# New tiling of a ConvNeXt block and a selective scan: sixteen-tile convolutions, tiled MLP, scan units of 1568 tokens

## The chip, the core and the metric

The kernel runs on one core of one Trainium2 chip. The metric is the time of one execution in microseconds (us) on the device. Engines are written as in the profile: PE (matrix engine; PEld is its weight load), DVE (vector), ACT (scalar/activation), POOL (GpSimd), SP (the queue that issues most DMAs). SBUF is the working memory of 128 partitions, PSUM the small memory that PE writes into, DRAM the large memory outside.

## The reference

The input `x` is 32 images of 96 channels, 56 by 56, in float32. Two layers follow each other:

```python
# layer 0
h = depthwise_conv7x7(x) + conv_b                       # per channel
h = (h - mean_c(h)) * rsqrt(var_c(h) + 1e-5) * g + b     # over the 96 channels
h = gelu(h @ w1 + b1) @ w2 + b2                          # 96 -> 384 -> 96
x = h * layer_scale + x
# layer 1, L = 3136 tokens per image, N = 4, R = 6
xs = silu(depthwise_conv5x5(x) + conv_b)
dts, Bs, Cs = split(x_proj_w @ xs)                       # 6, 4, 4 rows
delta = softplus(dt_w @ dts + dt_b)                      # 96 x L
log_dA = maximum(delta * A, log(1e-9))                   # 96 x 4 x L
P = exp(cumsum(log_dA)); dB_u = delta * Bs * xs
hs = P * cumsum(dB_u / maximum(P, 1e-9))
y = sum_n(hs * Cs) + xs * Ds
```

## The kernel before

The kernel has four stages, one after the other; each stage leaves its result in DRAM and the next one loads it.

**Convolution 1 (96 steps, one per channel).** `convolve` (L191) puts 112 image rows (2 half-batches of 56 rows) on the partitions and 16 images of 56 columns along the free side. The vertical part of the 7x7 filter is a banded 112x112 matrix, loaded for each channel from `taps_d` (L196); the horizontal part is seven shifted matmuls for each of two halves of 448 columns (L212). ACT adds the bias (L238), POOL's queue stores the result, and DVE with ACT accumulates the channel sums and squares (L245 to L248). After the last channel DVE and ACT make `rstd`, which goes to DRAM.

**MLP (112 steps, one per image row).** SP loads 96x896 tiles of the convolution, of `rstd` and of `x`; DVE multiplies by `rstd` (L273); PE does three times two matmuls into `ph` (L278), ACT the Gelu (L286), PE three times two matmuls into `po` (L293), DVE the residual sum (L301).

**Convolution 2** is like convolution 1 with five taps and a Silu (L316).

**Scan (384 units).** A unit is 784 tokens of one image (a quarter) times 32 of the 96 channels times 4 states, that is 128 partitions. An order written out by hand and pinned (`pin`) interleaves the steps of neighbouring units. `spread_du` copies 32 rows of `du` four times with four DMAs (L415, from SBUF to SBUF); `decay` makes the decay factor on ACT in three passes (L424 to L426); `drive` (L431) and `weigh` (L458) are products on POOL, `delta_x` (L392) a third one per quarter image; `scan` runs three operations on DVE: a scan into `run` (L439), a `min` and product in place in `run` (L446), and a second scan (L450). `gather` sums the states on PE (L468), `store` copies the result out on ACT (L477) and SP stores it. These lines decide where the DVE's operands lie (`ps_k` is a pool in PSUM):

```python
pv = ps_k.tile([128, 1024], F32, name="pv")
nc.vector.memset(pv, 0.0)
zero = pv[:, 1023:1024].to_broadcast([128, CH])
run = pv[:, :CH]
```

Of the kernel before, what the change touches and what calls it, by code (L numbers as in the profile page):

```python
# [15 lines left out]
B2, BI = 2, 16  # L16
ROWS = B2 * H
COLS = BI * W
HALF = COLS // 2
# [4 lines left out]
WP = 2 * H - 1  # L24
CH = 784
NCH = L // CH
BK = CH // 2
LN_EPS = 1e-5
EPS = 1e-9
DG = C // 3  # L30
# [4 lines left out]
def convnext_then_scan_kernel(  # L35
# [22 lines left out]
    nc = tc.nc  # L58
    const = ctx.enter_context(tc.tile_pool(name="const", bufs=1))
    dram = ctx.enter_context(tc.tile_pool(name="dram", bufs=1, space=DRAM))  # L60


    conv1_d = dram.tile([C, ROWS, COLS], F32, name="conv1_d")
    block_d = dram.tile([C, ROWS, COLS], F32, name="block_d")
    conv2_d = dram.tile([C, ROWS, COLS], F32, name="conv2_d")
    rstd_d = dram.tile([ROWS, COLS], F32, name="rstd_d")
    taps1_d = dram.tile([C, WP * K1], F32, name="taps1_d")
    taps2_d = dram.tile([C, WP * K2], F32, name="taps2_d")

# [5 lines left out]
    def across(src, parts, n, name):  # L75
        t = const.tile([parts, n], F32, name=name)
        nc.sync.dma_start(t, src.rearrange("(o n) -> o n", o=1).to_broadcast([parts, n]))
        return t


# [5 lines left out]
    nc.gpsimd.memset(lift_t[:, 0:1], -EPS)  # L86
    nc.gpsimd.memset(lift_t[:, 1:2], EPS)

    c1b_t = across(c1b, ROWS, C, "c1b_t")
    c2b_t = across(c2b, ROWS, C, "c2b_t")  # L90
    g_t = column(ln_g, C, "g_t")
    lnb_t = column(ln_b, C, "lnb_t")
    b2_t = column(b2, C, "b2_t")
    ls_t = column(ls, C, "ls_t")
    ls_b = across(ls, 128, C, "ls_b")
    dtb_t = column(dtb, C, "dtb_t")
    ds_t = column(ds, C, "ds_t")
    w1_t = const.tile([C, F], F32, name="w1_t")
    nc.sync.dma_start(w1_t, w1)
# [4 lines left out]
    xp_t = const.tile([R, C], F32, name="xp_t")  # L104
    nc.sync.dma_start(xp_t, xp[:R, :])
    xpT_t = const.tile([C, R + 2 * N], F32, name="xpT_t")
    nc.sync.dma_start(xpT_t, xpT)
    dtwT_t = const.tile([R, C], F32, name="dtwT_t")
    nc.sync.dma_start(dtwT_t, dtwT)
    a_t = const.tile([128, NG], F32, name="a_t")  # L110
    for n in range(N):
        nc.sync.dma_start(
            a_t[n * DG : (n + 1) * DG, :],
            alog[n * C : (n + 1) * C].rearrange("(g p) -> p g", p=DG),
        )

    w1c_t = const.tile([C, F], F32, name="w1c_t")
    b1p_t = const.tile([128, 3], F32, name="b1p_t")
    b2p_t = const.tile([C, 1], F32, name="b2p_t")
    wd_t = const.tile([C, C], F32, name="wd_t")  # L120
    bcw_t = const.tile([C, 32], F32, name="bcw_t")
    pick_t = const.tile([128, 128], F32, name="pick_t")
    sel_t = const.tile([128, DG], F32, name="sel_t")
    dsm_t = const.tile([C, C], F32, name="dsm_t")

    with tc.tile_pool(name="prep", bufs=1) as prep, tc.tile_pool(
        name="prep_ps", bufs=1, space=PSUM
    ) as prep_ps:

        for taps_d, cw, k, flip in ((taps1_d, c1w, K1, False), (taps2_d, c2w, K2, True)):  # L130
            kt = prep.tile([C, k * k], F32, name=f"kt{k}")
            nc.sync.dma_start(kt, cw)
            pad = prep.tile([C, WP * k], F32, name=f"pad{k}")
            nc.vector.memset(pad, 0.0)
            at = (H - 1 - k // 2) * k
            if flip:
                for i in range(k):
                    j = k - 1 - i
                    nc.vector.tensor_copy(
                        pad[:, at + i * k : at + (i + 1) * k], kt[:, j * k : (j + 1) * k]  # L140
                    )
            else:
                nc.vector.tensor_copy(pad[:, at : at + k * k], kt)
            nc.sync.dma_start(taps_d, pad)


        cen = prep.tile([C, C], F32, name="cen")
        nc.vector.tensor_scalar(cen, ident[:C, :C], -1.0 / C, None, ALU.add)
        w1g = prep.tile([C, F], F32, name="w1g")
        nc.vector.tensor_scalar(w1g, w1_t, g_t, None, ALU.mult)  # L150
        ps = prep_ps.tile([C, 512], F32, name="ps_w1")
        nc.tensor.matmul(ps[:, :F], lhsT=cen, rhs=w1g, start=True, stop=True)
        nc.vector.tensor_copy(w1c_t, ps[:, :F])
# [7 lines left out]

# [4 lines left out]
        ps = prep_ps.tile([C, 512], F32, name="ps_wd")  # L166
        nc.tensor.matmul(ps[:, :C], lhsT=xp_t, rhs=dtwT_t, start=True, stop=True)
        nc.vector.tensor_copy(wd_t, ps[:, :C])


        nc.vector.memset(bcw_t, 0.0)
        nc.vector.tensor_copy(bcw_t[:, : 2 * N], xpT_t[:, R:])
        nc.vector.memset(pick_t, 0.0)
        for k in range(4):
            rows = slice(32 * k, 32 * k + 2 * N)
            for n in range(N):
                at = 32 * k + (k // 2) * N + n
                nc.vector.tensor_copy(
                    pick_t[rows, n * DG : (n + 1) * DG],
                    ident[rows, at : at + 1].to_broadcast([2 * N, DG]),  # L180
                )
        for n in range(N):
            rows = slice(n * DG, (n + 1) * DG)
            nc.vector.tensor_copy(sel_t[rows], ident[rows, rows])
# [3 lines left out]

    def convolve(src, taps_d, k, pool, psum, wts, c, load):  # L191
        wt = wts[c % len(wts)]
        for j in range(B2):
            rows = slice(j * H, (j + 1) * H)
            taps = bass.AP(taps_d.tensor, taps_d.offset + c * WP * k, [[k, H], [1, H * k]])
            load.dma_start(  # L196
                wt[rows, j * H * k : (j + 1) * H * k],
                taps,
            )
# [21 lines left out]
    def two(t):  # L221
        return t.rearrange("p (s q) -> p s q", s=2)
# [341 lines left out]
```

## Time and profile before

| | us |
|---|---|
| median of 3 runs | 5092.57 (5092.25 to 5094.79) |
| span of the profiled execution, first to last instruction | 5088.6 |
| PE busy / DVE busy / ACT busy / POOL busy | 4048.3 / 2414.6 / 2311.2 / 1786.0 |
| first matmul of convolution 1, of the MLP, of convolution 2 | 23.9, 1032.1, 2054.6 |
| first DVE scan | 2797.8 |

For the profiled execution only its span is listed, not a time of its own; the span lies 4.0 us below the median. Busy times are unions: where matmuls overlap, PE is counted once. A line of the profile's groups reads: line, engine, operation, output from inputs by their names, shapes, count, then busy time, mean duration of one in ns, and the idle time just before with what ended it. DMA share is the mean busy share of 16 DMA engines. Every float32 matmul of the program appears as two records (4608 for the 2304 of L212); such a record is called a pass below.

### The profile page before, as it was taken

How to read it: one execution, taken by the hardware profiler on the slowest of the kernel's cores; microseconds unless marked ns; L12 is line 12 of the kernel's file. 1: busy time of each engine (PE TensorE's matmuls, PEld its weight loads, DVE VectorE, ACT ScalarE, POOL GpSimd, SP SyncE). 2: the span in 40 equal slices, each digit the busy share in tenths (PEclk: the TensorE clock that was granted, in tenths of full speed). 3: DMA queues.
4: the chain of work that ended last, by engine and by line, in shares of the span. 5: the costliest groups of instructions: out<-in, count | busy, mean ns of one | idle time of the engine just before them, and what ended most of it. 6: DMA issues, size and time to landing. Idle time of an engine off the chain costs nothing.

```text
span 5088.6 us, 38136 instructions
## 1 busy us (share of the span) xinstructions
PE 4048.3 (80%) x11914; PEld 2152.7 (42%) x11914; DVE 2414.6 (47%) x2004; ACT 2311.2 (45%) x2547; POOL 1786.0 (35%) x1209
## 2 busy tenths in 40 slices
PE   8999999989999999999998555555555555555555
PEld 6777777644444444677775111111111111111111
DVE  2333333322222222000000788778877787778878
ACT  1111111233333333111112777777777777777776
POOL 0000000000000000000001676767766676767766
PEclk9999999999999999999999777777777777777777
DMA  3333333255555544344445787777877787778875
GB/s 91 95 98 94 99 93 100 79 161 152 155 154 152 154 152 133 114 129 126 125 128 128 168 174 170 164 169 171 175 160 169 166 176 167 163 168 173 174 165 127
DMA packets 375571, 726.55 MB, mean 143 GB/s; under 512 B 220600, under 2 KB 242200, under 8 KB 375368
## 3 DMA queue, kind: packets, MB, share of 16 engines
q1 hardware_dynamic: 352840, 608.48, 52.0%
q0 software_dynamic: 22528, 115.62, 5.7%
q8 instruction: 95, 1.56, 0.1%
q14 instruction: 108, 0.88, 0.1%
HBM read 260.59 MB, written 155.05 MB: 82 GB/s over the span
## 4 chain that ended last, share of the span: by engine, by line
PE 21%; POOL 10%; DMA 7%; ACT 7%; DVE 5%; SPq 5%; issue 5%; POOLq 0%; ACTq 0%; DVEq 0%
PE ps L212 14%; DMA rep<-du 7%; POOL hc L458 5%; SPq L415 5%; POOL u L431 4%; PE pn L383 2%; PE py L468 2%; PE py L365 2%; DVE pv L439 2%; DVE hs L450 2%; ACT da L424 1%; ACT da L425 1%; DVE pv L446 1%; ACT L424 1%; POOL du L392 1%
## 5 line engine op out<-in xcount | busy, mean ns | idle before, releaser
L212 PE MATMUL ps<-xt,wt 112*112 112x440 f32 (+3 forms) x4608 | 1692.2, 530 | 21.0 <-DMA xt<-in_x_dram 11.3
L212 PEld LDWEIGHTS ps<-xt,wt 112*112 112x112 f32 x4608 | 1262.7, 274 | 450.3 <-issue 27.8
L365 PE MATMUL py<-xs,dsm_t 96*96 96x392 f32 x512 | 373.3, 884 | 842.9 <-ACT y L477 842.9
L431 POOL TENSOR_TENSOR u<-rep,bt 128x784 f32<-128x784 f32 x384 | 713.0, 1857 | 663.3 <-ACT bt L406 595.7
L458 POOL TENSOR_TENSOR hc<-hs,ct 128x784 f32<-128x784 f32 x384 | 712.1, 1854 | 9.9 <-DVE hs L450 9.9
L439 DVE TENSOR_TENSOR_SCAN pv<-da,cp,pv 128x784 f32<-128x784 f32 x288 | 534.2, 1855 | 375.3 <-ACT da L426 354.3
L286 ACT ACTIVATE g<-ph,b1p_t 128x896 f32<-128x896 f32 x336 | 338.7, 1008 | 676.1 <-PE ph L278 676.1
L365 PEld LDWEIGHTS py<-xs,dsm_t 96*96 96x96 f32 x512 | 122.4, 269 | 1047.5 <-ACT y L477 952.2
L468 PE MATMUL py<-hc,sel_t 128*32 128x392 f32 x1536 | 535.7, 571 | 16.7 <-POOL hc L458 16.7
L278 PE MATMUL ph<-h,w1c_t 96*128 96x448 f32 x1344 | 525.6, 540 | 25.2 <-DVE h L273 25.2
L450 DVE TENSOR_TENSOR_SCAN hs<-da,hs,pv 128x784 f32<-128x784 f32 x288 | 532.0, 1847 | 10.3
L293 PE MATMUL po<-g,w_t 128*96 128x448 f32 x1344 | 523.6, 539 | 0.0
L273 DVE TENSOR_TENSOR h<-h,r 96x896 f32<-96x896 f32 x112 | 121.8, 1088 | 734.4 <-DMA h<-conv_d 720.6
L304 POOL DMA_DIRECT2D block_d<-o x112 | 57.6, 514 | 980.5 <-DVE o L301 932.8
L446 DVE SCALAR_TENSOR_TENSOR pv<-pv,u 128x784 f32<-128x784 f32 x384 | 377.4, 983 | 40.8 <-DVE cp L444 0.5
L424 ACT ACTIVATE da<-rep,a_t 128x784 f32<-128x784 f32 x384 | 364.3, 949 | 67.5 <-DMA rep<-du 58.3
L245 DVE TENSOR_TENSOR dt<-ht,first 112x896 f32<-112x896 f32 x95 | 103.8, 1093 | 580.2 <-ACT ht L238 580.2
L278 PEld LDWEIGHTS ph<-h,w1c_t 96*128 96x128 f32 x1344 | 255.7, 190 | 279.8 <-issue 279.8
L241 POOL DMA_DIRECT2D conv_d<-ht x95 | 50.1, 527 | 919.9 <-ACT ht L238 919.9
L425 ACT ACTIVATE da<-da,lift_t 128x784 f32<-128x784 f32 x384 | 364.9, 950 | 12.5
L426 ACT ACTIVATE da<-da,lift_t 128x784 f32<-128x784 f32 x384 | 364.9, 950 | 12.5
L316 ACT ACTIVATE st<-ps,c2b_t 112x896 f32<-112x896 f32 x96 | 96.7, 1008 | 601.9 <-PE ps L212 601.9
(74 smaller groups left out, 2905.1 us busy)
## 6 DMA issues: line engine op xcount, KB each, us to landing
rep<-du SPq DMA_DIRECT2D x1536, 196.0 KB
xt<-in_x_dram SPq DMA_DIRECT2D x96, 392.0 KB
h<-conv_d SPq DMA_DIRECT2D x112, 336.0 KB
r<-rstd_d SPq DMA_DIRECT2D x112, 336.0 KB
x<-in_x_dram SPq DMA_DIRECT2D x112, 336.0 KB
block_d<-o POOLq DMA_DIRECT2D x112, 336.0 KB, 4.3
xt<-block_d SPq DMA_DIRECT2D x96, 392.0 KB
conv_d<-st POOLq DMA_DIRECT2D x96, 392.0 KB, 4.4
```

The lines of the kernel that those rows point to most:

```text
L212: nc.tensor.matmul(pv[:, :, lo:hi], lhsT=wv[:, :, kw], rhs=xv[:, s * (BI // 2) : (s + 1) * (BI // 2), lo + dx : hi + dx], start=(i == 0), ...
L278: nc.tensor.matmul(ph[:, s, :HALF], lhsT=w1c_t[:, f * 128 : (f + 1) * 128], rhs=ht[:, s * HALF : (s + 1) * HALF], start=True, stop=True,)
L293: nc.tensor.matmul(po[:, s, :HALF], lhsT=w2_t[:, f, :], rhs=gs[f][:, s * HALF : (s + 1) * HALF], start=(f == 0), stop=(f == 2),)
L365: pin(nc.tensor.matmul(ps[:, s, :BK], lhsT=wt, rhs=xt[:, s * BK : (s + 1) * BK], start=start, stop=stop,))
L424: pin(nc.scalar.activation(da, reps[i][:, 0, :], AF.Exp, scale=a_t[:, g : g + 1]))
L425: pin(nc.scalar.activation(da, da, AF.Relu, bias=lift_t[:, 0:1], scale=1.0))
L431: pin(nc.gpsimd.tensor_mul(ut, reps.pop(i)[:, 1, :], bts[i // NG]))
L439: pin(nc.vector.tensor_tensor_scan(run, da, zero, carry["p", g] if q else 1.0 / EPS, ALU.mult, ALU.add))
L446: pin(nc.vector.scalar_tensor_tensor(run, in0=run, scalar=1.0, in1=ut, op0=ALU.min, op1=ALU.mult))
L450: pin(nc.vector.tensor_tensor_scan(ht, da, run, carry["h", g] if q else 0.0, ALU.mult, ALU.add))
L458: pin(nc.gpsimd.tensor_mul(hc, done.pop(i), cts[i // NG]))
L468: pin(nc.tensor.matmul(pys[k][g * DG : (g + 1) * DG, s, :BK], lhsT=sel_t, rhs=hc[:, s * BK : (s + 1) * BK], start=False, stop=True, tile_p ...
```

## The change

All four stages get another tiling.

- **Convolutions:** 48 tiles instead of 96 channels. A tile is 8 images (one of 4 groups, `g`) times 8 channels (`kb`). PE is addressed as 16 tiles of 32 by 32: row tile `i` holds 31 input rows of a half image and a row of ones for the bias, column tile `j` another channel. For each tap there are 16 matmuls with `tile_position`. The filter matrices of all 12 `kb` are loaded once, by `weights`, with 96 DMAs on ACT's queue in each convolution; each second one overwrites the last row of what the one before it wrote. The input tile is loaded by eight DMAs of 16 or 15 partitions each.
- **Statistics** stay in SBUF (`rstd_t`) and are spread over partitions by a matmul (`rb`).
- **MLP:** 56 units of four image rows of 8 images. The first product is done as 32x128 row tiles (three thirds `e` of the channels accumulate), the second as 128x32 column tiles.
- **Scan:** 192 units of 1568 tokens. `fetch` loads the spread `delta` and `delta*x` from DRAM with two DMAs of 128 partitions, after `delta` and `delta_x` wrote them there; `decay` has two ACT passes instead of three; every product writes over one of its inputs; `run` and the zero operand lie in SBUF.

The core of the diff:

```diff
+    def weights(t, taps_d, bias_d, k, n, kb, zs):
+        for i in range(Q):
+            cp, h = divmod(i, 2)
+            c0 = kb * 8 + cp
+            pin(nc.scalar.dma_start(
+                t[i * PR : (i + 1) * PR],
+                at(taps_d, c0 * n * k + zs[h] * k, [[k, PR], [2 * n * k, Q], [1, PR * k]]),
+            ))
+            pin(nc.scalar.dma_start(
+                t[i * PR + PR - 1 : (i + 1) * PR],
+                at(bias_d, c0 * PR * k, [[PR * k, 1], [2 * PR * k, Q], [1, PR * k]]),
+            ))
+
+    def convolve(ps, xt, wt, k):
...
+            for i in range(Q):
+                rows = slice(i * PR, (i + 1) * PR)
+                for j in range(Q):
+                    cols = slice(j * PR, (j + 1) * PR)
+                    pv = ps[cols, i, :COLS].rearrange("p (b w) -> p b w", w=W)
+                    pin(nc.tensor.matmul(
+                        pv[:, :, lo:hi],
+                        lhsT=wv[rows, j, :, kw],
+                        rhs=xv[rows, j, :, lo + dx : hi + dx],
+                        start=(t == 0),
+                        stop=(t == k - 1),
+                        tile_position=(i * PR, j * PR),
+                    ))
...
+        wts = []
+        for kb in range(KB):
+            wt = keep.tile([128, Q, PR * K1], F32, name=f"wt1_{kb}")
+            weights(wt, taps1_d, bias1_d, K1, T1, kb, (3, 0))
+            wts.append(wt)
+        xts = [keep.tile([128, Q, COLS], F32, name=f"x1_{i}") for i in range(4)]
...
+            for i in range(Q):
+                cp, h = divmod(i, 2)
+                for lo, hi in pieces():
+                    row = g * H + h * LOW + lo
+                    pin(nc.sync.dma_start(
+                        xt[i * PR + lo : i * PR + hi],
+                        at(x, ((kb * 8 + cp) * ROWS + row) * COLS,
+                           [[COLS, hi - lo], [2 * ROWS * COLS, Q], [1, COLS]]),
+                    ))
+        for n in range(B2 * KB):
+            g, kb = divmod(n, KB)
+            if n + 3 < B2 * KB:
+                load1(n + 3)
+            ps = psum.tile([128, Q, 512], F32, name=f"ps1_{n}", tag="ps")
+            convolve(ps, xts[n % len(xts)], wts[kb], K1)
+            ht = pool.tile([128, Q, COLS], F32, name=f"ht_{n}", tag="ht", bufs=3)
+            pin(nc.scalar.copy(ht, ps[:, :, :COLS]))
+            sq = pool.tile([128, Q, COLS], F32, name=f"sq_{n}", tag="sq")
+            pin(nc.scalar.activation(sq, ht, AF.Square))
...
+            for q in range(Q):
+                m = o * Q + q
+                rows = slice(q * PR, (q + 1) * PR)
+                for e in range(3):
+                    pin(nc.sync.dma_start(
+                        ht[rows, e].rearrange("p h w -> p (h w)"),
+                        at(conv1_d[g], (e * 16 * PR + m) * SLOT,
+                           [[PR * SLOT, 16], [2 * COLS, 2], [1, 2 * COLS]]),
+                    ))
...
+            for e in range(3):
+                for q in range(Q):
+                    rows = slice(q * PR, (q + 1) * PR)
+                    pin(nc.tensor.matmul(
+                        ph[:, q, :COLS], lhsT=w1c_t[rows, e, f * 128 : (f + 1) * 128],
+                        rhs=ht[rows, e, h], start=(e == 0), stop=(e == 2),
+                        tile_position=(q * PR, 0),
+                    ))
+            gt = pool.tile([128, Q, COLS], F32, name=f"g_{u}_{f}", tag="g", bufs=6)
+            pin(nc.scalar.activation(
+                gt, ph[:, :, :COLS], AF.Gelu, bias=b1p_t[:, f : f + 1], scale=1.0
+            ))
...
+                for q in range(Q):
+                    rows = slice(q * PR, (q + 1) * PR)
+                    pin(nc.tensor.matmul(
+                        po[rows, e, :COLS], lhsT=w2_t[:, f, e * PR : (e + 1) * PR],
+                        rhs=gts[u, f][:, q], start=(f == 0), stop=(f == 2),
+                        tile_position=(0, q * PR),
+                    ))
...
-        pv = ps_k.tile([128, 1024], F32, name="pv")
-        nc.vector.memset(pv, 0.0)
-        zero = pv[:, 1023:1024].to_broadcast([128, CH])
-        run = pv[:, :CH]
...
+            pin(nc.sync.dma_start(dl_d[k], dl))
...
-        def spread_du(i):
-
+            for i, (home, name) in enumerate(((bts, "bt"), (cts, "ct"))):
+                pk = psum.tile([128, Q, 512], F32, name=f"pk_{k}_{i}", tag="bc")
+                spread(pk, pick_t[:, i, :], k, 128)
+                t = pool.tile([128, T], F32, name=f"{name}_{k}", tag=name)
+                pin(nc.scalar.copy(four(t), pk[:, :, :BK]))
+                home[k] = t
+
+        def fetch(i):
             k, g = divmod(i, NG)
-            rep = pool.tile([128, 2, CH], F32, name=f"rep_{i}", tag="rep", bufs=4)
-            for n in range(N):
-                pin(nc.sync.dma_start(
-                    rep[n * DG : (n + 1) * DG], dus[k][g * DG : (g + 1) * DG]
-                ))
-            reps[i] = rep
+            da = pool.tile([128, T], F32, name=f"da_{i}", tag="da", bufs=6)
+            ut = pool.tile([128, T], F32, name=f"u_{i}", tag="u", bufs=6)
+            for t, d in ((da, dl_d[k]), (ut, dx_d[k])):
+                pin(nc.sync.dma_start(t, at(d, g * PR * T, [[T, PR], [0, N], [1, T]])))
+            das[i], us[i] = da, ut
 
         def decay(i):
-
-            k, g = divmod(i, NG)
-            da = pool.tile([128, CH], F32, name=f"da_{i}", tag="da", bufs=5)
-            pin(nc.scalar.activation(da, reps[i][:, 0, :], AF.Exp, scale=a_t[:, g : g + 1]))
-            pin(nc.scalar.activation(da, da, AF.Relu, bias=lift_t[:, 0:1], scale=1.0))
-            pin(nc.scalar.activation(da, da, AF.Identity, bias=lift_t[:, 1:2], scale=1.0))
-            ready[i] = da
+            da, g = das[i], i % NG
+            pin(nc.scalar.activation(
+                da, da, AF.Relu, bias=lift_t[:, 0:1], scale=a_t[:, g : g + 1]
+            ))
+            pin(nc.scalar.activation(da, da, AF.Exp, bias=lift_t[:, 1:2], scale=1.0))
 
         def drive(i):
-            ut = pool.tile([128, CH], F32, name=f"u_{i}", tag="u", bufs=5)
-            pin(nc.gpsimd.tensor_mul(ut, reps.pop(i)[:, 1, :], bts[i // NG]))
-            ready[i] = ready[i], ut
+            pin(nc.gpsimd.tensor_mul(us[i], us[i], bts[i // NG]))
 
         def scan(i):
             k, g = divmod(i, NG)
-            q = k % NCH
-            da, ut = ready.pop(i)
-
+            q = k % 2
+            da, ut = das[i], us[i]
+            run = pool.tile([128, T], F32, name=f"run_{i}", tag="run", bufs=1)
             pin(nc.vector.tensor_tensor_scan(
                 run, da, zero, carry["p", g] if q else 1.0 / EPS, ALU.mult, ALU.add
             ))
-            if q < NCH - 1:
+            if q == 0:
                 cp = pool.tile([128, 1], F32, name=f"cp_{i}", tag=f"cp{g}")
-                pin(nc.vector.tensor_copy(cp, run[:, CH - 1 : CH]))
+                pin(nc.vector.tensor_copy(cp, run[:, T - 1 : T]))
                 carry["p", g] = cp
             pin(nc.vector.scalar_tensor_tensor(
-                run, in0=run, scalar=1.0, in1=ut, op0=ALU.min, op1=ALU.mult
-            ))
-            ht = pool.tile([128, CH], F32, name=f"hs_{i}", tag="hs", bufs=5)
+                ut, in0=run, scalar=1.0, in1=ut, op0=ALU.min, op1=ALU.mult
+            ))
             pin(nc.vector.tensor_tensor_scan(
-                ht, da, run, carry["h", g] if q else 0.0, ALU.mult, ALU.add
-            ))
-            carry["h", g] = ht[:, CH - 1 : CH]
-            done[i] = ht
+                ut, da, ut, carry["h", g] if q else 0.0, ALU.mult, ALU.add
+            ))
+            carry["h", g] = ut[:, T - 1 : T]
...
         def weigh(i):
-            hc = pool.tile([128, CH], F32, name=f"hc_{i}", tag="hc", bufs=3)
-            pin(nc.gpsimd.tensor_mul(hc, done.pop(i), cts[i // NG]))
-            done[i] = hc
-
-        def gather(i):
-            k, g = divmod(i, NG)
+            pin(nc.gpsimd.tensor_mul(das[i], us.pop(i), cts[i // NG]))
+            hcs[i] = das.pop(i)
```

The main loop of the scan now does, at step `i`: `fetch(i + 4)`, `decay(i + 2)`, `drive(i + 2)`, `scan(i)`, `weigh(i - 1)`, `gather` of unit `i - 2`.

## Prediction

> **What bounds the kernel now.** I read the stages first: four windows cut at the first matmul of each stage and the first DVE scan.
>
> ```profile
> core 0: us, PE busy (x) PEld busy (x) DVE busy (x) ACT busy (x) POOL busy (x), PEclk, DMA share, GB/s
> 0.00:1032.00 1032.00, 986.67 (x2698) 747.56 (x2698) 331.80 (x337) 192.27 (x196) 51.57 (x105) 0.99 0.33 94
> 1032.00:2055.00 1023.00, 1013.17 (x2689) 475.08 (x2690) 249.01 (x227) 338.71 (x336) 57.59 (x112) 1.00 0.49 151
> 2055.00:2798.00 743.00, 728.61 (x1988) 523.86 (x1987) 1.08 (x2) 110.66 (x113) 61.67 (x102) 0.98 0.45 126
> 2798.00:5088.60 2290.60, 1319.85 (x4540) 406.25 (x4540) 1832.71 (x1440) 1669.56 (x1903) 1615.21 (x890) 0.74 0.77 167
> ```
>
> In the first three stages PE is busy 96 to 99% at full clock and everything else at most half: PE is the bound. The scan has no engine that is always busy; DVE comes first with 1832.7 of 2290.6. There DVE and POOL together are busy 3447.9 us, so for at least 1157 us both work at once. The groups by line give the price of each operation:
>
> ```profile
> L212 PE MATMUL ps<-xt,wt 112*112 112x440 f32 (+3 forms) x4608 | 1692.2, 530 | 21.0 <-DMA xt<-in_x_dram 11.3
> ...
> L431 POOL TENSOR_TENSOR u<-rep,bt 128x784 f32<-128x784 f32 x384 | 713.0, 1857 | 663.3 <-ACT bt L406 595.7
> L458 POOL TENSOR_TENSOR hc<-hs,ct 128x784 f32<-128x784 f32 x384 | 712.1, 1854 | 9.9 <-DVE hs L450 9.9
> L439 DVE TENSOR_TENSOR_SCAN pv<-da,cp,pv 128x784 f32<-128x784 f32 x288 | 534.2, 1855 | 375.3 <-ACT da L426 354.3
> ...
> L278 PE MATMUL ph<-h,w1c_t 96*128 96x448 f32 x1344 | 525.6, 540 | 25.2 <-DVE h L273 25.2
> L450 DVE TENSOR_TENSOR_SCAN hs<-da,hs,pv 128x784 f32<-128x784 f32 x288 | 532.0, 1847 | 10.3
> ...
> L446 DVE SCALAR_TENSOR_TENSOR pv<-pv,u 128x784 f32<-128x784 f32 x384 | 377.4, 983 | 40.8 <-DVE cp L444 0.5
> ```
>
> Matmul passes overlap, so I use busy time over count: 1692.2/4608 = 0.367 us per pass in the convolutions, 525.6/1344 = 0.39 in the MLP (0.375 where nothing waits: the timeline has runs of 12 passes in 4.67 us, 11 x 0.375 and one whole pass of 0.54). In the scan rows look at the operands: each of the three DVE operations has one of its two tensors in `pv`, which is PSUM, even the zero of L439. Last, two stretches of the timeline (start, duration, what). The first, of the scan, shows whether tiles of PE run side by side; `pk` is four row tiles, `py` a column tile:
>
> ```profile
> 4009.61 0.94 PE L400 MATMUL pk<-bn,pick_t 8*128 8x392 f32 x8
> ...
> 4010.49 0.86 PE L468 MATMUL py<-hc,sel_t 128*32 128x392 f32 x4
> ```
>
> The second, of the start, shows what it costs when a DMA waits for another to land:
>
> ```profile
> 15.07 0.79 SPq L144 DMA_DIRECT2D taps_d<-pad  x2
> 17.69 0.74 SPq L196 DMA_DIRECT2D wt<-taps_d  x2
> ```
>
> Eight passes in four row tiles take 0.94 us, where one after the other they would take 8 x 0.33 = 2.6. Sixteen passes of `pn` in four column tiles (L383, at 4049.81) take 2.75 us at a low clock, against 5.2 at the full one. So tiles overlap four-fold, both ways; of sixteen at once there is no row.
>
> **The change, stage by stage.** I call one set of passes that run side by side a round.
>
> *Convolution 1.* Now 2688 passes x 0.367 = 987 us on PE. After: 48 tiles x 7 taps x 2 passes = 14 rounds of 0.367 = 5.1 us per tile, if 16 tiles overlap as 4 do. The other engines per tile: ACT one copy (L406: 807 ns for 784 columns, so under 1.9 for 1792) and a Square (952 ns for 896, under 1.9), DVE four additions of 896 (1093 ns each, 4.4 us), all below the DMA. A tile loads 0.89 MB and stores 0.92 MB. Two rows give the rate at full DMA share: 94/0.33 = 285 GB/s where a transfer covers 112 partitions, 167/0.77 = 217 in the scan, where `rep` goes into 32. The packets agree: 6272 bytes of `rep` take 239 ns at the 5th percentile, but 479 in the median. The new loads cover 16 or 15 partitions; no row shows that. Bounds per tile: 1.81 MB at 285 = 6.3 us; loads at half of 217 (8.2) plus store at 285 (3.2) = 11.4. I take 9.0, nearer to the `rep` row, with the store mostly beside the loads. PE then idles part of the time; at the clock of 0.74 that the scan row grants it would need 6.9 us, still hidden. The skill's page "SBUF — State Buffer", section "Door 1: The DMA port swizzle", lists 104 GB/s for partitions 0 to 15; by it the loads alone would be an estimated 8.5 us.
>
> New, and on the path: the 96 weight DMAs stand on ACT's queue ahead of the first copy, and each second one overwrites a row of the one before, so it waits for its landing. The row: issue 0.37, then 1.83 us from the end of the `taps_d` issue to the next that waits for it, then 0.37: 2.6 us a pair, 48 pairs = 125 us (2.2 to 3.0 a pair: 106 to 144). Behind them wait ACT's copies, and PE, which has two PSUM buffers and stops after two tiles. The `x` loads on SP hide under it. Sum: 24 lead-in (as now) + 125 + 47 x 9.0 + 26 lead-in of the MLP (as now) + 12 for three rounds of statistics = **610** (464 to 742), now 1032.
>
> *MLP.* Per unit 9 rounds for the first and 9 for the second product, two passes each: 36 passes x 0.375 = 13.5, `rb` 0.75. Six changes between row and column tiles: above, 0.88 us pass from the first `pk` to the next `py` where two rounds are 0.65, so 0.1 to 0.23 each; I take 0.15 = 0.9. That is 15.1 us x 56 = 846, + 10 to the next stage = **856** (805 to 884), now 1023. ACT's Gelu (under 2.0 us) has `ph` in one buffer and hides under the other product's 2.2 us; without that cover it would add 3 x 2 us per unit, 336 us. DMA: 4.1 MB per two units at 217 GB/s = 19 of 30 us, hidden.
>
> *Convolution 2.* PE 10 rounds, 3.7 us; DMA as above. The weights' DMAs now wait on ACT behind the last Gelu and for the buffers of the MLP: 125 + 47 x 9.0 + 34 to the first scan (as now) = **582** (436 to 714), now 743.
>
> *Scan.* ACT loses the third pass; two of under 1.9 us and a third of the copies and the softplus make at most 6.1 us per unit, hidden, and its whole sum, 1170 us, would still lie below DVE's. SP's 1536 copies become 384 loads from DRAM; the way out and back is waited for once, 30 us. The two engines that matter keep their elements, at half the instructions. The fixed part of one is at most what its smallest takes: DVE 158 ns (L444, one column), POOL 100 (a memset of one column). DVE per unit: 2 x (2 x 1855 - 158) + (2 x 983 - 158) + 80 = 8.99 us. POOL: 3.61 us x 2 1/3 (`drive`, `weigh`, a third of `delta_x`) = 8.43 us.
>
> The open cost is whether these still overlap, since now **both tensors of all three DVE operations lie in SBUF**, as do POOL's. No row shows such a pair: the two-SBUF additions L245 to L248 run while POOL only issues DMAs. Bounds: full overlap as in today's rows, 8.99 us per unit; no overlap, 17.42. The rows lean to the second: POOL, which takes both its tensors from SBUF, needs 1857 ns for what DVE does in 983 with one of them in PSUM, as if it had one way for both; and the overlap seen holds for a DVE that reads SBUF once. So 192 x 17.42 + 30 + 11 (end) = **3386** (16.7 per unit if the fixed parts overlap, 18.1 if every duration doubles: 3247 to 3516), now 2291.
>
> The rule that speaks against the change stands on the same page, section "Who interferes with whom": a DVE instruction with two SBUF inputs and a GpSimd instruction that reads SBUF exclude each other for the whole instruction. Today's trace does not contradict it (1157 us of overlap, always with a PSUM operand), and no run here shows it yet; by it the stage is the longer sum, by the overlap rows alone the shorter.
>
> Together 610 + 856 + 582 + 3386 = 5434 against the span of 5088.6; with the 4 us around the span **5438**. The three stages before the scan gain 750 us, the scan gives back 1095.
>
> **The rivals.**
>
> *DVE and POOL overlap as now* (the other side). The scan then needs DVE's 8.99 x 192 = 1726 at least; today's stage is 1.25 times its DVE time, which would be 2157, and DMA (462 MB at 217 GB/s) 2130. With 2100 + 41 the total is 4190. For it: the means of L439 and L458 today show no stretching. It decides below 15.6 us per unit: (5089 - 610 - 856 - 582 - 41)/192.
>
> *They hinder each other in part*, say half way, 13.2 us per unit: 2576, total 4630.
>
> *Sixteen tiles do not run at once.* If only four overlap, as seen, a tile of convolution 1 takes 56 x 0.367 = 20.6 us and one of convolution 2 14.7: 47 x (11.6 + 5.7) = 813 more, 6250. Against it: row tiles and column tiles each overlap fully, and passes start about 13 ns apart, 16 in 0.2 us.
>
> That the change does not do what it says I leave out: the order of instructions has 16 matmuls per tap and SBUF operands.
>
> **How the numbers follow.** No overlap 0.66, own range 4956 to 5860; overlap 0.13; in part 0.14; four tiles only 0.07. The first case ends below today's time only if nearly all of its terms fall to their low ends together: 0.07 faster, 0.01 same, 0.58 slower. The third gives 0.13 faster and 0.01 same. Faster 0.33, same 0.02, slower 0.65; about 0.2% is what a measurement of this kernel tells from no change. The range reaches from within the third case to the top of the first, 4450 to 5870, and leaves out the second and the fourth.
>
> **What would show it.** In the profile after: DVE's scans and POOL's products of 128x1568 not at 3.6 us but stretched, or alternating, with the sum of their undisturbed times near the stage's length; convolution tiles 9 us apart with PE idle for DMA; about 125 us at the start of each convolution in which ACT does nothing. Scan operations at 3.55 us with POOL busy beside them would prove the main step wrong, tiles 5 us apart the DMA step.

## The result and the profile after

The changed kernel takes 5152.6 us (median of 4 runs, 5144.4 to 5159.3), the kernel before 5092.4 in the same runs: a ratio of 1.0117, 95% interval 1.0103 to 1.0132. It is slower by 60 us where 345 were forecast. The profiled execution took 5147.2 us with a span of 5145.4. First the windows, cut at the first matmul of each stage and the first DVE scan as before:

```profile
core 0: us, PE busy (x) PEld busy (x) DVE busy (x) ACT busy (x) POOL busy (x), PEclk, DMA share, GB/s
0.00:638.00 638.00, 398.32 (x10798) 278.07 (x10798) 238.71 (x246) 171.42 (x107) 32.88 (x63) 0.84 0.57 151
638.00:1529.00 891.00, 868.07 (x8174) 328.11 (x8174) 208.75 (x336) 296.03 (x169) 125.58 (x228) 0.98 0.47 130
1529.00:2058.00 529.00, 291.71 (x7736) 191.26 (x7736) 0.32 (x1) 94.38 (x60) 35.53 (x51) 0.78 0.69 190
2058.00:5145.00 3087.00, 952.16 (x5064) 189.22 (x5064) 3056.19 (x672) 1069.34 (x758) 2509.92 (x446) 0.51 0.46 147
```

| stage | before | forecast | after |
|---|---|---|---|
| convolution 1 | 1032 | 610 | 638 |
| MLP | 1023 | 856 | 891 |
| convolution 2 | 743 | 582 | 529 |
| scan | 2291 | 3386 | 3087 |

The first three stages gain 740 us (750 forecast), the scan gives back 796 (1095 forecast). In the scan DVE is now busy for 3056 of 3087 us, where it was busy for 1833 before with the same elements to process; POOL is busy for 2510, and the two together for 5566 us. The chain of work that ended last names the same engine, and the groups of the page show what became of each instruction:

```profile
DVE 60%; PE 29%; issue 7%; DMA 2%; SPq 1%; ACT 0%; ACTq 0%; POOL 0%; POOLq 0%; DVEq 0%
```

```profile
L575 POOL TENSOR_TENSOR u<-u,bt 128x1568 f32<-128x1568 f32 x192 | 1032.9, 5380 | 502.1 <-DMA u<-dx_d 483.3
L598 POOL TENSOR_TENSOR da<-u,ct 128x1568 f32<-128x1568 f32 x192 | 1134.3, 5908 | 89.3 <-DVE u L592 89.3
L582 DVE TENSOR_TENSOR_SCAN run<-da,zero_t 128x1568 f32<-128x1568 f32 x96 | 662.7, 6903 | 541.8 <-DMA u<-dx_d 541.8
L589 DVE SCALAR_TENSOR_TENSOR u<-run,u 128x1568 f32<-128x1568 f32 x192 | 784.4, 4086 | 10.0
L592 DVE TENSOR_TENSOR_SCAN u<-da,u,u 128x1568 f32<-128x1568 f32 x96 | 565.1, 5887 | 3.4
```

Twice the columns would be 3.5 us for a scan and for a product, 1.8 us for L589. Every group of DVE and POOL is far above that, DVE almost without idle time. (The 541.8 us of idle time at L582 is DVE's wait in convolution 2, before the stage.) The last microseconds of the timeline (start, duration, what) show how the time arises; the fences hold DVE's lines and POOL's:

```profile
5118.89 3.48 DVE L592 TENSOR_TENSOR_SCAN u<-da,u,u 128x1568 f32<-128x1568 f32 x1
5122.29 3.46 DVE L582 TENSOR_TENSOR_SCAN run<-da,cp,zero_t 128x1568 f32<-128x1568 f32 x1
5125.86 4.82 DVE L589 SCALAR_TENSOR_TENSOR u<-run,u 128x1568 f32<-128x1568 f32 x1
5130.72 3.48 DVE L592 TENSOR_TENSOR_SCAN u<-da,u,u 128x1568 f32<-128x1568 f32 x1
```

```profile
5122.55 6.48 POOL L598 TENSOR_TENSOR da<-u,ct 128x1568 f32<-128x1568 f32 x1 [5.34 <-DVE u L592]
5134.37 3.48 POOL L598 TENSOR_TENSOR da<-u,ct 128x1568 f32<-128x1568 f32 x1 [5.34 <-DVE u L592]
```

At 5122.55 POOL starts a product while DVE scans. The scan keeps its 3.46 us and ends at 5125.75; the product ends at 5129.03, 3.28 us later. L589 starts at 5125.86, should take 1.8 us and ends at 5130.68, 1.65 us after the product. So whoever came first goes on undisturbed, and the other counts as busy while it stands. The last product, alone after DVE's end, takes 3.48 us. The records of the whole stage agree: of the 384 scans 112 take 3.4 to 3.5 us, 255 take 6.6 to 6.7, 16 take 10.1 or 13.5 and one takes 4.1; of the 192 of L589, 47 take 1.8 us and 145 take 4.8 to 4.9. DVE loses the time of whole products; if the two shared a rate, the durations between would be there too.

In the convolutions, the list of waits has the chain of weight transfers on ACT's queue, once for each (ACTq, further below, is that queue's issuing of DMAs):

```profile
ACT L477 <- DMA wt<-taps_d: 171.5, 1, 171.5
ACT ht L298 <- DMA wt<-taps_d: 157.4, 1, 157.4
```

PE does two tiles, then stands from 58.5 to 173.9 us, and from 1564.8 to 1679.3 in convolution 2. From there on, tiles follow each other by 9.46 us on the mean (435.3 us for 46 tiles) and by 7.08 us. The first mean holds three rounds of statistics, one after each 12 tiles, in which no tile is on PE for 9 to 10 us (28.8 us together); without them it is 8.84 us.

### The profile page after: what moved, and what is told of

Read it like the earlier page. It is cut to its first block, busy times and chain, and to the rows that moved or that the text cites. A ratio compares the mean times of both kernels' runs of the same rounds, so it can differ in the third digit from the quotient of the medians.

```text
span 5145.4 us, 72040 instructions
## 1 busy us (share of the span) xinstructions
PE 2510.3 (49%) x31772; PEld 986.7 (19%) x31772; DVE 3504.0 (68%) x1253; ACT 1631.2 (32%) x1093; POOL 2703.9 (53%) x787
## 4 chain that ended last, share of the span: by engine, by line
DVE 60%; PE 29%; issue 7%; DMA 2%; SPq 1%; ACT 0%; ACTq 0%; POOL 0%; POOLq 0%; DVEq 0%
DVE run L582 22%; DVE u L592 22%; DVE u L589 15%; PE ps L246 12%; PE ph L382 8%; PE po L404 8%; DMA wt<-taps_d 1%; PE rb L367 1%; PE pm L317 0%; DVE cp L587 0%; SPq L502 0%; DMA x<-block_d 0%; ACTq L228 0%; DMA u<-dx_d 0%; DMA x<-in_x_dram 0%
## 5 line engine op out<-in xcount | busy, mean ns | idle before, releaser
L575 POOL TENSOR_TENSOR u<-u,bt 128x1568 f32<-128x1568 f32 x192 | 1032.9, 5380 | 502.1 <-DMA u<-dx_d 483.3
L598 POOL TENSOR_TENSOR da<-u,ct 128x1568 f32<-128x1568 f32 x192 | 1134.3, 5908 | 89.3 <-DVE u L592 89.3
L582 DVE TENSOR_TENSOR_SCAN run<-da,zero_t 128x1568 f32<-128x1568 f32 x96 | 662.7, 6903 | 541.8 <-DMA u<-dx_d 541.8
L246 PE MATMUL ps<-x,wt 32*32 32x440 f32 (+3 forms) x18432 | 651.0, 585 | 398.1 <-issue 353.2
L589 DVE SCALAR_TENSOR_TENSOR u<-run,u 128x1568 f32<-128x1568 f32 x192 | 784.4, 4086 | 10.0
L246 PEld LDWEIGHTS ps<-x,wt 32*32 32x32 f32 x18432 | 454.0, 141 | 595.7 <-issue 514.8
L592 DVE TENSOR_TENSOR_SCAN u<-da,u,u 128x1568 f32<-128x1568 f32 x96 | 565.1, 5887 | 3.4
L592 DVE TENSOR_TENSOR_SCAN u<-da,u 128x1568 f32<-128x1568 f32 x96 | 547.8, 5706 | 3.3
L582 DVE TENSOR_TENSOR_SCAN run<-da,cp,zero_t 128x1568 f32<-128x1568 f32 x96 | 504.6, 5256 | 0.0
L382 PE MATMUL ph<-h,w1c_t 32*128 32x448 f32 x4032 | 434.6, 560 | 22.7 <-DVE h L373 16.4
```

What stands on the lines that cost most here:

```text
L246: pin(nc.tensor.matmul(pv[:, :, lo:hi], lhsT=wv[rows, j, :, kw], rhs=xv[rows, j, :, lo + dx : hi + dx], start=(t == 0), stop=(t == k - 1), ...
L382: pin(nc.tensor.matmul(ph[:, q, :COLS], lhsT=w1c_t[rows, e, f * 128 : (f + 1) * 128], rhs=ht[rows, e, h], start=(e == 0), stop=(e == 2), t ...
L575: pin(nc.gpsimd.tensor_mul(us[i], us[i], bts[i // NG]))
L582: pin(nc.vector.tensor_tensor_scan(run, da, zero, carry["p", g] if q else 1.0 / EPS, ALU.mult, ALU.add))
L589: pin(nc.vector.scalar_tensor_tensor(ut, in0=run, scalar=1.0, in1=ut, op0=ALU.min, op1=ALU.mult))
L592: pin(nc.vector.tensor_tensor_scan(ut, da, ut, carry["h", g] if q else 0.0, ALU.mult, ALU.add))
```

## The experiments

My theory was the prediction's main step: a DVE instruction with two tensors in SBUF and a POOL product exclude each other while they stream. The rivals were that DVE is slow by itself in its new form (a unit twice as long, work in place, the fetch from DRAM), or that the two only share a rate; the durations above, which come in steps of a whole product, speak against the second.

**1. The exclusion alone, in the kernel before.** Nothing but the home of two operands changes:

```diff
-        pv = ps_k.tile([128, 1024], F32, name="pv")
-        nc.vector.memset(pv, 0.0)
-        zero = pv[:, 1023:1024].to_broadcast([128, CH])
-        run = pv[:, :CH]
+        zero_t = pool.tile([128, 1], F32, name="zero_t", bufs=1)
+        nc.vector.memset(zero_t, 0.0)
+        zero = zero_t.to_broadcast([128, CH])
+        run = pool.tile([128, CH], F32, name="run", bufs=1)
```

> The kernel before, with only the scan's `run` and `zero` moved from PSUM to SBUF; tiling, units of 784 tokens and copies unchanged. Exclusion (a DVE instruction with both tensors in SBUF and a POOL product wait for each other while they stream): a unit becomes about the sum of DVE's 4.69 us and POOL's 4.33 us, 9.0 us, less what the fixed parts of some five instructions overlap (up to 1.0 us), so 8.0 to 9.0 x 384 = 3070 to 3460 us for the scan against 2291, and 5870 to 6260 in all; L439 and L450 stretch from 1.85 us to over 2.5. No exclusion (the larger unit, the work in place or the way through DRAM slows the changed scan): 5092 within 1%, L439 at 1.85 us. Half hindrance: about 5500.

Measured: 6001.8 us, a ratio of 1.179 [1.176, 1.181]. The scan goes from 2291 to 3203 us, 8.34 us a unit. The groups of this run:

```profile
L458 POOL TENSOR_TENSOR hc<-hs,ct 128x784 f32<-128x784 f32 x384 | 1204.8, 3138 | 653.5 <-DVE hs L450 572.2
L446 DVE SCALAR_TENSOR_TENSOR run<-run,u 128x784 f32<-128x784 f32 x384 | 850.4, 2215 | 41.1 <-DVE cp L444 0.9
L439 DVE TENSOR_TENSOR_SCAN run<-da,cp,zero_t 128x784 f32<-128x784 f32 x288 | 844.6, 2933 | 30.8 <-DVE hs L450 0.9
```

983 ns became 2215 for L446, 1855 became 2933 for L439 and 3138 for L458. Unit size, work in place and the fetch are as they were, so the operands alone make a loss of 910 us. Whether the larger unit, the work in place or the fetch add to it in the changed kernel is what experiment 4 shows.

**2. One operand of one column.**

```diff
-        zero = pv[:, 1023:1024].to_broadcast([128, CH])
+        zero_t = pool.tile([128, 1], F32, name="zero_t", bufs=1)
+        nc.vector.memset(zero_t, 0.0)
+        zero = zero_t.to_broadcast([128, CH])
```

> The kernel before, with only `zero`, one column read with stride 0, moved from PSUM to SBUF; `run` stays in PSUM. Only the first scan (L439) then has both of its inputs in SBUF. Exclusion, if one column read over and over counts as an SBUF input: L439 stretches from 1.85 us to 2.5 or more and POOL's 4.33 us and 1.85 us exclude each other, 6.2 us a unit against 5.96: between 5092 and 5350. If such an operand does not count, or if nothing excludes: 5092 within 0.5% and L439 at 1.85 us.

Measured: 5193.1 us, 1.020 [1.018, 1.022]. In the groups of this run (its lines lie two lower), the scan into `run` stretches although it still writes to PSUM and its second input is one column read 784 times; the two operations that keep a PSUM input stay at 983 and 1847 ns:

```profile
L441 DVE TENSOR_TENSOR_SCAN pv<-da,cp,zero_t 128x784 f32<-128x784 f32 x288 | 774.3, 2689 | 224.2 <-ACT da L428 200.1 <-DVE hs L452 0.5
L452 DVE TENSOR_TENSOR_SCAN hs<-da,hs,pv 128x784 f32<-128x784 f32 x288 | 532.0, 1847 | 10.3
L448 DVE SCALAR_TENSOR_TENSOR pv<-pv,u 128x784 f32<-128x784 f32 x384 | 377.3, 983 | 41.2 <-DVE cp L446 0.9 <-DVE pv L441 0.5
```

So it is the inputs that count, the output does not free them, and a repeated column counts as an input.

**3. Less POOL work beside the same DVE work.** The product with C is left out, and `gather` takes `us[i]` in its place:

```diff
-            pin(nc.gpsimd.tensor_mul(das[i], us.pop(i), cts[i // NG]))
-            hcs[i] = das.pop(i)
+            das.pop(i)
+            hcs[i] = us.pop(i)
```

> The changed kernel without `weigh`: the product with C on POOL is left out, and PE takes the scan's output itself. DVE's work is untouched. Exclusion: each unit gives back the product's streaming time, 3.0 to 3.5 of 16.0 us, so 192 x 12.5 to 13.0 us and 4490 to 4580 in all; the DVE scans shorten with nothing done to them. DVE slow by itself (the larger unit, in place, the fetch): 5150 as before, scans still at 5.3 to 6.9 us.

Measured: 4567.6 us; 12.98 us a unit (scan from 2066.0 to 4557.9 us) against 16.08.

**4. No POOL work at all.** As experiment 3, and also:

```diff
-            dx = pool.tile([C, T], F32, name=f"dx_{k}", tag="dx")
-            pin(nc.gpsimd.tensor_mul(dx, dls.pop(k), tokens(k)))
-            pin(nc.sync.dma_start(dx_d[k], dx))
+            dls.pop(k)
+            pin(nc.sync.dma_start(dx_d[k], tokens(k)))
...
-            pin(nc.gpsimd.tensor_mul(us[i], us[i], bts[i // NG]))
+            pass
```

> The changed kernel without any product on POOL: it leaves out `drive`, `weigh` and the product in `delta_x` (the tokens go to dx_d as they are). DVE's work is untouched. Exclusion: nothing stretches any more, scans at 3.5 us, L589 at 1.8; 8.9 to 9.1 us a unit, a scan of 1720 to 1790 us and 3780 to 3850 in all. DVE slow by itself: scans at 5.3 us or more, over 4900. Bound by the fetch from DRAM: DVE waits for DMA, and the unit stays above 10 us.

Measured: 3747.6 us, 8.77 us a unit, a little under the expected band. The groups of this run give DVE's undisturbed durations:

```profile
L588 DVE SCALAR_TENSOR_TENSOR u<-run,u 128x1568 f32<-128x1568 f32 x192 | 344.1, 1792 | 8.9 <-PE pz L528 0.4
L591 DVE TENSOR_TENSOR_SCAN u<-da,u,u 128x1568 f32<-128x1568 f32 x96 | 334.5, 3484 | 3.4
L581 DVE TENSOR_TENSOR_SCAN run<-da,cp,zero_t 128x1568 f32<-128x1568 f32 x96 | 332.1, 3459 | 0.0
```

DVE is not slow by itself: that rival is out. Experiments 3 and 4 and the changed kernel make a straight line. A unit costs 8.77 us without products, 12.98 with 1.33 of them and 16.08 with 2.33: 3.16 us for each of the first, 3.10 for the last. A product takes 3.48 us alone, so about nine tenths of it are added to the unit.

**5. The products on DVE.** The same edit in `drive`, `weigh` and `delta_x`:

```diff
-            pin(nc.gpsimd.tensor_mul(us[i], us[i], bts[i // NG]))
+            pin(nc.vector.tensor_mul(us[i], us[i], bts[i // NG]))
```

> The changed kernel with all three products moved from POOL to DVE; nothing is left out. If the two engines exclude each other, POOL's help is worth less than nothing, since a product takes 3.48 us there and about 1.8 us on DVE (L589): a unit becomes 8.9 + 2.33 x 1.8 = 13.1 us, the scan 2560 us, 4620 in all. If DVE is slow by itself, at 5.3 to 6.9 us a scan: 16 + 4.2 = 20 us a unit, over 5900.

Measured: 4696.5 us, 0.922 [0.918, 0.927]. Without any help from POOL the kernel is 456 us faster than the changed one. The unit is 13.63 us, 0.5 above the forecast. DVE stands idle for 207.1 us before L575, 181.9 of them within the stage, that is 0.95 a unit, mostly for the fetch; its busy time, 12.58 us a unit, lies under the forecast:

```profile
L575 DVE TENSOR_TENSOR u<-u,bt 128x1568 f32<-128x1568 f32 x192 | 342.9, 1786 | 207.1 <-DMA u<-dx_d 196.8
```

**6. New convolutions and MLP, old scan.** The scan of the kernel before with its constants is put behind the three new stages; only its `load` has to change:

```diff
-            pin(nc.sync.dma_start(
-                xt.rearrange("p (h w) -> p h w", w=W),
-                conv2_d[:, j * H : (j + 1) * H, i * W : (i + 1) * W],
-            ))
+            for cp in range(2):
+                for h in range(2):
+                    pin(nc.sync.dma_start(
+                        xt[cp::2, h * T : (h + 1) * T].rearrange("p (r w) -> p r w", w=W),
+                        at(conv2_d[g], (cp * 2 + h) * COLS + i * W,
+                           [[PR * SLOT, KJ], [SLOT, HH], [1, W]]),
+                    ))
```

> The changed kernel's convolutions and MLP, with the scan of the kernel before (784 tokens a unit, `run` and `zero` in PSUM) that loads its tokens from the new layout of conv2_d. If the loss sits in the scan alone, and the stages do not disturb each other: the changed kernel's 2058 us up to the first scan plus 2291, about 4350 (4300 to 4450). If the new layout of conv2_d also costs the scan, or the gain in the first stages was only work put off: above 4500.

Measured: 4351.8 us, 0.855 [0.853, 0.856]. The first DVE scan starts at 2056.6, the scan takes 2292. The loss is in the scan alone, and the gain before it is real.

**7. The chain of weight transfers, a first try.** The bias row overwrites the last row of the taps, so the taps get one row less:

```diff
-                t[i * PR : (i + 1) * PR],
-                at(taps_d, c0 * n * k + zs[h] * k, [[k, PR], [2 * n * k, Q], [1, PR * k]]),
+                t[i * PR : (i + 1) * PR - 1],
+                at(taps_d, c0 * n * k + zs[h] * k, [[k, PR - 1], [2 * n * k, Q], [1, PR * k]]),
```

> The changed kernel with the taps written to 31 rows of each tile, so that the bias row no longer overwrites a part of them and the 96 DMAs of a convolution need not wait for each other. If the chain of waits is what holds the first tiles: a pair takes the two issues of 0.5 us instead of 3.1, the chain shrinks by some 100 us in each convolution, 4960 in all (4930 to 5000). If the loads that fill up meanwhile would be late anyway: 5100 or more.

Measured: 5319.5 us, a miss to the other side: 167 us slower than the changed kernel. PE now stands until 290.7 us instead of 173.9. The stretch from 40 to 60 us of this run, one digit or number per half microsecond (DMA share in tenths, GB/s), then ACT's queue in the timeline:

```profile
DMA  0000001530000000003500000000106100000000
GB/s 23 22 25 22 22 23 25 108 131 14 23 22 23 23 22 23 23 27 70 186 9 22 23 22 23 23 23 22 29 22 192 41 20 22 23 22 23 23 23 22
```

```profile
25.34 5.49 ACTq L228 DMA_DIRECT2D wt<-bias_d  x1
30.87 0.42 ACTq L224 DMA_DIRECT2D wt<-taps_d  x1
31.34 5.17 ACTq L228 DMA_DIRECT2D wt<-bias_d  x1
```

The waits for a landing are gone, but the queue is blocked for over 5 us a pair, and the transfers crawl at 22 to 23 GB/s. That is 124 runs of 896 bytes at 41 ns, one after the other, as a single DMA engine would do them (in these 20 us the queue's packets take 6.7% of 16 engines, about one); the transfer of 32 rows went through in about 1.1 us. The Trainium skill, page "DMA: Bandwidth & Descriptors", section "Why a DMA increments its semaphore by 16 and not by 1", has the rule: the engines used are the largest number up to 16 that divides the slowest dimension. 31 is prime; the run agrees. The premise, that the waits were the cost, was neither shown nor refuted by this run.

**8. The chain, second try, on the hybrid.** The four taps' DMAs of a group of channels go first, then its four bias DMAs, so that a bias row waits for a transfer four places back; only three groups stand ahead of the loop, the others are issued tile by tile:

```diff
+        for i in range(Q):
+            c0 = kb * 8 + i // 2
             pin(nc.scalar.dma_start(
                 t[i * PR + PR - 1 : (i + 1) * PR],
...
+            if kb < 3:
-            weights(wt, taps1_d, bias1_d, K1, T1, kb, (3, 0))
+                weights(wt, taps1_d, bias1_d, K1, T1, kb, (3, 0))
...
             convolve(ps, xts[n % len(xts)], wts[kb], K1)
+            if n + 3 < KB:
+                weights(wts[n + 3], taps1_d, bias1_d, K1, T1, n + 3, (3, 0))
```

> The hybrid (new convolutions and MLP, old scan) with the weights' DMAs in another order: only those of the first three groups of channels stand ahead of the loop, four taps' DMAs and then their four bias DMAs, and each tile issues those of the third group after it. The transfers are the same. If the chain of waits on ACT's queue is what holds PE after two tiles: the two gaps of 115 us close but for some 15 us each, 4352 - 200 = 4150 (4110 to 4200). If the loads of x set the pace and the stall only hid them: 4300 or more.

Measured: 4166.8 us (4130.5 to 4170.4), 0.816 [0.813, 0.819]: the fastest version. PE has no gap over 12 us left in either convolution, and the first DVE scan comes at 1876.4 instead of 2056.6 us: 90 us saved in each convolution. The chain was on the path. Not all of the standstill is gained: in convolution 1 the tiles behind it stand 10.3 us apart on the mean, 9.6 in the hybrid of experiment 6. How much is due to the order of a group's DMAs and how much to issuing them tile by tile is not separated.

**9. What sets the pace of the tiles.** The changed kernel, in both convolutions:

```diff
-            if n + 3 < B2 * KB:
+            if n + 3 < len(xts):
```

> The changed kernel with only the first four tiles of each convolution loaded; the later tiles compute on old data, so the output is wrong and 88 tiles' loads are left out. Tiles now follow each other by 9.5 us in convolution 1 and 7.1 in convolution 2. Loads set this, and PE's rounds go at 0.367 us when fed: 5.2 and 3.7 us a tile, about 4790 in all. PE sets it with rounds of 0.565 us: 7.9 and 5.65 us, about 5010. The store or ACT sets it: no change, 5150.

Measured: 4981.8 us. The tiles follow each other by 7.46 and 5.56 us instead of 9.46 and 7.08: the loads add 2.0 and 1.5 us a tile, PE sets the rest, near the second of the three expectations. (Without the rounds of statistics, 27.7 us here, convolution 1 has 6.9 us a tile.) The windows of this run between the gap and the last matmul show PE busy 95 and 91% of the time at full clock:

```profile
171.00:513.00 342.00, 325.13 (x10314) 256.43 (x10298) 212.60 (x189) 162.03 (x100) 24.53 (x47) 0.98 0.33 130
1577.00:1832.00 255.00, 231.64 (x7356) 172.16 (x7336) 0.00 (x0) 75.73 (x46) 24.65 (x47) 0.99 0.43 171
```

PE hardly waits for the loads themselves: in the changed kernel its waits for a landing of `x` behind the standstill are 0 and 3.1 us. What it has instead are short idle times with no wait that the profile shows ("issue"), nearly all after 126 to 128 passes or a multiple of that (a tile of convolution 1 has 224, one of convolution 2 has 160):

```profile
290.23 4.35 PE L246 MATMUL ps<-x,wt 32*32 32x424 f32 x126 [0.92 <-issue]
295.76 4.15 PE L246 MATMUL ps<-x,wt 32*32 32x440 f32 x128 [1.19 <-issue]
```

In the trace's records of the changed kernel I count 46 such times in convolution 1 and 48 in convolution 2 behind the standstill (0.3 to 8 us each, 58.8 and 66.6 us together), without the loads 5 and 22 (4.2 and 22.5 us): 1.2 of the 2.0 and 1.0 of the 1.5 us a tile. Nearly all end 1.2 to 1.8 us after a packet of 16384 bytes has landed on the queue that the page calls "q8 instruction" (250 packets, 4.10 MB). So the loads seem to hold up PE's supply of instructions. The word "issue" alone would not tell, since the standstill of 115 us carries it too; the number of passes and the landings do. No run changes that supply alone, so this is a reading of the trace and is not shown by an experiment.

**10. Columns or instructions.** The same with every tap but the middle one on half the images:

```diff
+                    m = BI if t == 0 else BI // 2
...
-                        pv[:, :, lo:hi],
+                        pv[:, :m, lo:hi],
...
-                        rhs=xv[rows, j, :, lo + dx : hi + dx],
+                        rhs=xv[rows, j, :m, lo + dx : hi + dx],
```

> As the run with the loads done once, and in addition every tap but the middle one takes only four of a tile's eight images, so 6 of 7 and 4 of 5 rounds stream half the columns; half of the other taps' work is left out. The tiles stood 7.46 and 5.56 us apart there, 0.53 to 0.56 us a round of sixteen matmuls and sixteen weight loads. If columns streamed through PE set the round: 8/14 and 6/10 of it, 4.3 and 3.3 us a tile, about 250 us less, 4730 in all. If handing out the 32 instructions of a round sets it (17 ns each): no change, 4980.

Measured: 4983.5 us, unchanged, with tiles 7.98 and 5.18 us apart and PE busy for less of the time (254.5 of 342 us). The number is that of the second expectation, but the reason given there is not what the trace shows. First a stretch of experiment 9, then one of this run:

```profile
269.48 27.48 PE L246 MATMUL ps<-x,wt 32*32 32x448 f32 x906
```

```profile
284.35 2.98 PE L247 MATMUL ps<-x,wt 32*32 32x220 f32 x128 [1.15 <-issue]
288.07 2.60 PE L247 MATMUL ps<-x,wt 32*32 32x212 f32 x128 [0.74 <-issue]
291.53 2.98 PE L247 MATMUL ps<-x,wt 32*32 32x216 f32 x128 [0.85 <-issue]
```

With all columns PE runs on without a gap, 906 passes in 27.48 us, 0.485 us for a round of 16. With half the columns 128 passes take 2.60 to 2.98 us, 0.33 to 0.37 a round, so columns do cost; but then PE stands for about a microsecond, mostly after 128 passes with their 128 weight loads, and goes on about 1.4 us after a packet has landed on the instruction queue. The supply of instructions, it seems, takes over as the limit where the columns no longer are. That no run changes it alone holds here too.

## Why the prediction was right or wrong

**The main step held.** The prediction chose "no overlap" between DVE and POOL against today's 1157 us of overlap, and named the operands as the reason. Experiments 1 to 4 and the durations in steps of a product show it. The rival of full overlap (4190) is out, and so is the half-way one: a product's cost is added almost whole. The sign was right by little, though: 60 us are 0.31 us a unit, and had the unit taken that much less, the change would have gained. The section of the skill that the prediction weighed ("SBUF — State Buffer", "Who interferes with whom") holds for scans and repeated columns too; but not quite for "the whole instruction", since 3.1 of 3.48 us are excluded.

**The step that failed is the size of the scan's unit: 17.42 us forecast, 16.08 measured**, 192 x 1.34 = 257 of the 289 us by which the sum missed. Since a gain of 750 and a loss of 1095 us were set against each other, this 8% turned a difference of 345 us into one of 60. Of the 1.34, 0.53 is that the instructions alone are shorter than the sum took them (DVE 8.77 and not 8.99 us, experiment 4; a product 3.48 and not 3.61); the other 0.81 is overlap that the sum put at nothing. The 41 us added for the way out and back and for the end did not come on top either: the measured unit is the whole stage over 192. The forecast unit is the sum of whole durations, and the prediction's own low end, 16.7, took the fixed parts to be 158 ns (DVE) and 100 ns (POOL). Two sizes of the same operation, undisturbed, give them better (the short ones with one input of DVE in PSUM). From 784 to 1568 columns POOL's product goes from 1.855 to 3.48 us, so 1568 columns stream in 3.25 us and 0.23 are fixed; DVE's scan goes from 1.84 (mean of its groups before) to 3.44 (experiment 4), L589 from 0.98 to 1.79, so they stream in 3.21 and 1.62 with some 0.2 fixed. Streaming parts alone: 2 x 3.21 + 1.62 + 2.33 x 3.25 = 15.6 us; whole durations, with 0.08 for L587, 16.9. The measured 16.08 lies between, nearer to the first: streams exclude each other, and part of one engine's fixed time runs beside the other's stream. The working with fixed parts is an account that fits, not shown by an experiment of its own. The fixed part read from an instruction with one column was too small, and the low end of the scan's range, 3247 us, rested on it; 3087 came out.

**The other stages** missed by +28, +35 and -53 us, which nearly cancel. In convolution 1 the chain of 48 pairs took 150 us (first to third tile) against 125, since a pair took 3.1 us and not 2.6. What follows took 435.3 us where 47 x 9.0 + 12 = 435 were forecast, and that was luck: the prediction had PE at 5.1 us a tile, hidden under the loads, and it needs 6.9 (experiment 9); the loads added the rest, by the trace not through their own landing. The price of a round was the mis-sized part: 0.367 us is the row of one pass on the undivided array, taken to hold for 16 tiles as it does for four, and 16 took 0.485 without a gap. The Trainium skill comes nearer: "TensorE: Matmul & The Clock Gate", section "Measured speedup vs the span model", gives 10.6 times for 4x4 tiles, an estimated 16 x 0.367 / 10.6 = 0.55 us, above the measured 0.485. The rival "sixteen tiles do not run at once" was therefore right in a small part. In convolution 2 the tile took 7.08 against 9.0, 47 x 1.9 = 90 us less; its chain took 25 us more than forecast, and from its last matmul to the first scan it took 52 us and not 34. Over those tiles 249 GB/s moved at a DMA share of 0.88, which is 283 at a full share: the rate of the row for 112 partitions (285) and not half of 217, as I had leaned to for transfers of 16 and 15 partitions. The 104 GB/s of the skill's "Door 1" did not bind either, with eight such transfers to different partitions for each tile (0.89 MB in 7.08 us are 125 GB/s for the loads alone); one alone was not measured.

**The MLP** took 891 against 856: PE was busy 868 us over 56 units, 15.5 us each where 15.1 were forecast, at full clock; 23 us more it was idle. That part was right.

## What to carry to other kernels

Before moving an operand of a DVE instruction from PSUM to SBUF, look at what POOL does meanwhile: with two SBUF inputs on DVE, work given to POOL is added to DVE's time, and a product is cheaper on DVE (1.8 against 3.1 us here). Where two engines exclude each other, add their streaming parts, with the fixed part taken from two sizes of the same operation: here that gave 15.6 us, whole durations 16.9, and 16.08 came out. A change that rewrites all stages should be judged stage by stage: the new convolutions and MLP with the old scan and shorter weight queues take 18% less time than the kernel before, though the whole change made it slower.

## What the runs showed of the hardware that I had not expected

A transfer of 31 partitions ran at 22 GB/s where one of 32 took about 1.1 us for nearly the same bytes. A stride-0 input of one column excludes POOL like a whole tensor. And with matmuls on sixteen tiles of 32x32 PE seems to run out of instructions (read from the trace, not tested by a run of its own): a round took 0.485 us for 440 columns and 0.33 to 0.37 for half of them, but with half of them PE stood after most runs of 128 passes for about a microsecond, until some 1.4 us after 16384 bytes had landed on the instruction queue.
